# Masked attention with a residual: bulk loads and stores split over the slots, turns moved ahead, an If with its sides exchanged

## The chip, the cores and the metric

The kernel runs on one core of one Trainium2 chip, in one launch. The metric is device time in microseconds. A core has five engines that run their own instruction streams: TensorE (PE, with its weight loads as PEld), VectorE (DVE), ScalarE (ACT), GpSimd (POOL) and SyncE (SP). DMAs are issued by SP, ACT and POOL, in the order of their own streams, and moved by 16 DMA engines.

## The reference, cut to what matters

```python
def ref(x, mask, Wq, Wo):            # x (8, 512, 1024), mask (8, 1024) of 0 and 1
    NH = 8; B, D, T = x.shape; dk = D // NH
    xt = transpose(x, (0, 2, 1))
    q = xt @ Wq.T
    qh = q.reshape(B, T, NH, dk).transpose(0, 2, 1, 3)
    scores = einsum('bhqd,bhkd->bhqk', qh, qh) / sqrt(dk)
    logits = (scores * cmask + (1 - cmask) * -1e30) * rmask
    attn = softmax(logits)
    ctx = einsum('bhqk,bhkd->bhqd', attn, qh)
    out = ctx.transpose(0, 2, 1, 3).reshape(B, T, D) @ Wo.T
    return x + transpose(out, (0, 2, 1))
```

Queries, keys and values are the same projection. About half of the 1024 tokens of each batch are kept by the mask. A row that is masked out has equal logits everywhere, so its attention is the mean over all tokens.

## The kernel before, in words

Only the kept tokens are worked on. `early()` ranks the tokens by prefix sums of the mask and finds for each place of a packed list which token goes there. A value read from the chip (`fit`, the largest number of places that a batch needs) chooses a side of an If: `late(SHORT)` for up to 544 places, `late(LONG)` for up to 576. This input takes the short side. (Behind both stands another If with a slow version for all tokens, which is not entered.)

`late(n)` is one long schedule written out by hand. The work is cut into 32 pairs `(b, pr)`: batch b = 0 to 7 and four pairs of heads pr = 0 to 3. Each pair has five steps k = 0 to 4, one block of keys each; below, a slot (pr, k) of batch b is that step. In each slot TensorE does the scores of one block and then whatever the dictionaries and `slots_of` put there: the projection of a later pair, the attention of the pair before, blocks of the output projection. The order of the calls in the source is the order of the instructions on each engine, so a DMA's place in the source fixes its place on the issuing engine's queue, not its time.

What a batch needs beside the matmuls, and where it stood before:

- `load_batch(b + 2)`, L378: x as eight pieces of 256 KB in two tiles (tag `x`, two buffers), all on SP at slot (3, 0) of batch b.
- `turn(b + 1, i)`, L426 and L434: VectorE transposes a quarter of x to rows of tokens (`xt`, two buffers); four stores on SP put it to the DRAM tile `xd`. Slots (0, 0), (0, 1), (0, 3), (1, 0) of batch b.
- `add_features`, `mean_of`: ScalarE and VectorE sum x for the mean.
- `search(b + 2, i)`, `load_ranks`: which tokens are kept. `gather(b + 1, i)`, L494: GpSimd fetches the kept rows from `xd` into `xin`, slots (1, 3) and (1, 4). `collect`, L507: TensorE transposes them to `xc` at (2, 1) and (2, 2).
- `invert`, L728 to L753, at k = 0 of every pair: VectorE inverts the sums of the softmax (`rt`), four tiny stores `row<-rt` on SP, then two loads `rb<-row` on SP that wait for those stores. `contexts`, L763 to L772, multiplies with `rb` on VectorE at k = 4.
- `lengths_of` (`len`, `top`, VectorE, L586 and L593) and `bias_of` (L599 to L604, TensorE and VectorE): the largest length of the keys, needed before the next pair's scores can be exponentiated.
- `output`, L787: the output projection; `oc` goes by GpSimd to the DRAM tile `od`.
- `load_rest(b - 1)`, L857: x once more for the residual (`xr`, 2 MB in four DMAs of 512 KB, one buffer), on SP at (3, 4); at (2, 4) in the last batch.
- `fetch`, L899, and `finish_blocks`, L862 and L865: rows of `od` come back in token order, are transposed on VectorE and added to `xr`. After block 7 (and after block 3 for batch 6) the finished `xr` is stored to `out`, L872.

`issue_stores()` at the end of each slot issues the stores of `turn` at once and those of `finish_blocks` one slot later. The last batch's end is `fetch_last` and `finish_tokens`.

Of the kernel before, what the change touches and what calls it, by code (L numbers as in the profile page):

```python
# [10 lines left out]
F32 = mybir.dt.float32  # L11
# [10 lines left out]
Q = 32  # L22
SHORT = 544
# [282 lines left out]
def attention_of_kept_tokens(ctx, tc, x, mask, wq, wo, out, ident, wqT, woT, verdict, flag):  # L306


    nc = tc.nc
    B, D, T = x.shape  # L310
    P = 128
    DK = D // NH
    SCALE = 1.0 / math.sqrt(DK)
    ND = D // P
# [53 lines left out]
    xs, xbars, xmeans, xds, xins, xcs, parts, searches = {}, {}, {}, {}, {}, {}, {}, {}  # L368
    stores = [[], []]

    def load_batch(b, queue=None):

        features = x[b].rearrange("(p d) t -> d p t", d=ND)
        xs[b] = []
        for r in range(NN):
            xs[b].append(sb.tile([P, ND, NB], F32, tag="x", name=f"x_{b}_{r}", bufs=NN))
            for d in range(ND):
                (queue or nc.sync).dma_start(  # L378
                    xs[b][r][:, d, :], features[d][..., r * NB : (r + 1) * NB]
                )  # L380

    def queries_of(b):

# [11 lines left out]
    def turn_first(i):  # L395

        r, at = divmod(i * P, NB)
        pt = bank(f"xt_0_{i}")
        for d in range(ND):
            nc.tensor.transpose(pt[:, d * P : (d + 1) * P], xs[0][r][:, d, at : at + P], ident)  # L400
        if i == 0:
            xds[0] = dr.tile([T + 1, D], F32, tag="xd_0", name="xd_0", bufs=1)
            nc.gpsimd.dma_start(xds[0][T : T + 1, :], zero)
        tag = "oc" if i < NC else "xin"
        xt = sb.tile([P, D], F32, tag=tag, name=f"xt_0_{i}", bufs=NC)
        nc.scalar.copy(
            xt.rearrange("p (a d f) -> p a d f", a=A, d=ND),
            pt.rearrange("p (d a f) -> p a d f", d=ND, a=A),
        )
        nc.gpsimd.dma_start(xds[0][i * P : (i + 1) * P, :], xt)  # L410

    def mean_first():
        xbars[0] = keep.tile([P, ND, NN], F32, name="xbar_0")
# [359 lines left out]


    ods, gs, xrs = {}, {}, {}
    copies = []

    def output(b, i, wait=False):
        n = sizes[i]
# [71 lines left out]
    def in_blocks(t):  # L851
        return t.rearrange("(k f) (a n) -> a f k n", f=Q, a=A)

    def load_rest(b):
        xr = sb.tile([P, D // Q, T // A], F32, tag="xr", name=f"xr_{b}", bufs=1)
        for a in range(A):
            nc.sync.dma_start(xr[a * Q : (a + 1) * Q, :, :], in_blocks(x[b])[a])  # L857
        xrs[b] = xr

    def finish_blocks(b, i):  # L860
        o = sb.tile([P, D // Q, Q], F32, tag="o", name=f"o_{b}_{i}", bufs=2)
        nc.vector.transpose(o.rearrange("p k t -> p (k t)"), gs[b, i])  # L862
        xr = xrs[b]
        to = xr[:, :, i * Q : (i + 1) * Q]
        nc.vector.tensor_tensor(to, o, to, ALU.add)  # L865
        n = NT if b + 2 < B else G
        if (i + 1) % n == 0:
            cols = slice((i + 1 - n) * Q, (i + 1) * Q)

            def store():  # L870
                for a in range(A):
                    nc.sync.dma_start(  # L872
                        in_blocks(out[b])[a][:, :, cols], xr[a * Q : (a + 1) * Q, :, cols]
                    )

            stores[0].append(store)

    def fetch_last(b):

# [126 lines left out]
    def early():  # L1006
# [98 lines left out]
        mean_first()  # L1105
        for i in range(NC):
            search(0, i)
    def place_all():

        BC = B * NT  # L1110
        mrow, rank = seen["mrow"], seen["rank"]
        home, wrap = homes
        nc.vector.tensor_scalar(home, rank, float(-NK), None, ALU.add)
        nc.vector.tensor_tensor(home, home, mrow, ALU.mult)
        nc.vector.tensor_scalar(home, home, float(NK - 1 + END), None, ALU.add)
        nc.vector.tensor_scalar(wrap, home, float(NK), float(-NK), ALU.is_ge, ALU.mult)
        nc.vector.tensor_tensor(home, home, wrap, ALU.add)
# [8 lines left out]
    def late(n):  # L1126
        fit_to(n)
        nc.vector.tensor_scalar(lacks, kept, float(-NK), None, ALU.add)
        weights["wq"] = order_columns(load_weights(wq, "wq"), "wq")
        mean_of(0)  # L1130
        for i in range(NC):
            gather(0, i)
        queries_of(0)
# [16 lines left out]
        bias_of(pairs[0])  # L1150


        TURN = [(0, 0), (0, 1), (0, 3), (1, 0)]
        TURN_LATER = [(0, 2), (0, 4), (1, 0), (1, 1)]
        FEATURES = {(r, k): (r * G + k - 1, *((r * G + 3,) if k == 3 else ())) for r in range(NN) for k in (1, 2, 3)}
        SEARCH = {(2, 1): (0,), (2, 2): (1,), (2, 3): (2,), (2, 4): (3,), (3, 0): (4,)}
# [23 lines left out]
        FETCH_SOON = {**FETCH, (1, 3): (6,), (1, 4): (7,), (2, 0): (), (2, 1): ()}  # L1180
        FINISH_SOON = {**FINISH, (1, 4): (6, 7), (2, 2): (), (2, 3): ()}
        FETCH_LAST = {(2, k): (k,) for k in range(NC)} | {(3, k): (NC + k,) for k in range(NT - NC)}
        FINISH_LAST = {(3, 2): (0, 1), (3, 3): (2, 3), (3, 4): (4,)}
        for p, pair in enumerate(pairs):
            b, pr = pair
            before = pairs[p - 1] if p else None
            todo = slots_of(p)
            for k, c in enumerate(order):
                scores(pair, c)
                if k == (4 if p == ND - 1 else 3) and p + 1 < len(pairs):  # L1190
                    bias_of(pairs[p + 1])
                if k == 0 and p + 1 < len(pairs) and pairs[p + 1] in turned:
                    copy_values(pairs[p + 1])
                if k == 0:
                    for copy in copies:
                        copy()
                    copies.clear()
                if k == 1:
                    add_ends(pair)
                if k == 0 and before:  # L1200
                    if p + 1 < len(pairs):
                        invert(before)
                    else:
                        inv = inverses(before)
                if p + 1 == len(pairs):
                    if k == 1:
                        spread(before, inv)
                        contexts(before)
                elif k == 4 and before:
                    contexts(before)  # L1210
                if b + 1 < B:
                    at = TURN if b else TURN_LATER
                    if (pr, k) in at:
# [12 lines left out]
                if b + 2 < B:  # L1226
                    if pr == 3 and k == 0:
                        load_batch(b + 2)
                    if pr == 1 and k == 4:
                        load_ranks(b + 2)  # L1230
                    for i in SEARCH.get((pr, k), ()):
                        search(b + 2, i)
                if (pr, k) == ((3, 4) if b + 1 < B else (2, 4)) and b > 0:
                    load_rest(b - 1)
                if b > 1:
                    for i in (FETCH if b + 1 < B else FETCH_SOON).get((pr, k), ()):
                        keep_step(pair, c)
                        fetch(b - 2, i)
                if b + 1 == B:
                    for i in FETCH_LAST.get((pr, k), ()):  # L1240
                        keep_step(pair, c)
                        fetch(b - 1, i)
                if p == 0 and k == 1:
                    place_all()
                if p == 1 and k == 4:
                    turn_places()
                if p == ND - 1 and k < 2:
                    place_blocks(k)
                if b > 1:
                    for i in (FINISH if b + 1 < B else FINISH_SOON).get((pr, k), ()):  # L1250
                        finish_blocks(b - 2, i)
                if b + 1 == B:
                    for i in FINISH_LAST.get((pr, k), ()):
                        finish_blocks(b - 1, i)
                for task in todo[k]:
                    task()
                issue_stores()
            if p + 2 == len(pairs):
                attend_short(pair)
                for hf in range(2):  # L1260
                    attend_half(pair, hf)
# [50 lines left out]
def kernel(  # L1312
# [22 lines left out]
    with ExitStack() as pools:  # L1335
# [3 lines left out]
        with tc.manual_schedule():  # L1339
            early()  # L1340
        fit = nc.values_load(verdict[0:1, 0:1], min_val=0, max_val=2 * T)
        with tc.If(fit < SHORT) as short:
            with tc.manual_schedule():
                late(SHORT)
        with short.Else():
            with tc.If(fit < LONG):
                with tc.manual_schedule():
                    late(LONG)
    again = nc.values_load(flag[0:1, 0:1], min_val=0, max_val=1)
    with tc.If(again > 0):  # L1350
        turn_all_weights(tc, [(wq, wqT), (wo, woT)], ident)
# [29 lines left out]
```

## Time and profile before

| | |
|---|---|
| median of 3 runs | 726.82 us (723.42 to 730.56) |
| the profiled execution | 729.98 us, span 728.3 us, mean clock 0.949 |
| TensorE busy | 654.2 us, 90% of the span |
| VectorE, ScalarE, GpSimd busy | 359.2 us, 398.5 us, 184.4 us |
| moved by DMA | 116.43 MB, mean 160 GB/s |

The page of the profile cuts the span into 40 slices; a digit is the busy share of an engine in tenths. The view of waits lists which engine and line stood idle until which other instruction had ended: us in total, times, longest. The chain that ended last gives pieces in order of time: start, us, what. The timeline gives start, us, engine, line, operation and, in brackets, the idle time before it and what ended that. The view of windows gives for each stretch its length, the busy time (and count) of PE, PEld, DVE, ACT and POOL, the granted clock, the busy share of the DMA engines and GB/s. SPq is the queue of SyncE's DMA issues.

### The profile page before, as it was taken

How to read it: one execution, taken by the hardware profiler on the slowest of the kernel's cores; microseconds unless marked ns; L12 is line 12 of the kernel's file. 1: busy time of each engine (PE TensorE's matmuls, PEld its weight loads, DVE VectorE, ACT ScalarE, POOL GpSimd, SP SyncE). 2: the span in 40 equal slices, each digit the busy share in tenths (PEclk: the TensorE clock that was granted, in tenths of full speed). 3: DMA queues.
4: the chain of work that ended last, by engine and by line, in shares of the span. 5: the costliest groups of instructions: out<-in, count | busy, mean ns of one | idle time of the engine just before them, and what ended most of it. 6: DMA issues, size and time to landing. Idle time of an engine off the chain costs nothing.

```text
span 728.3 us, 12025 instructions
## 1 busy us (share of the span) xinstructions
PE 654.2 (90%) x4139; PEld 397.0 (55%) x4139; DVE 359.2 (49%) x1049; ACT 398.5 (55%) x1059; POOL 184.4 (25%) x311
## 2 busy tenths in 40 slices
PE   6689999999999995899959999699987999999962
PEld 5656666565556553565535656356554655554431
DVE  6147646253575434564364632935437333723461
ACT  5457678465765566265653558356682555544400
POOL 4620310310343013330224104240132301333040
PEclk9789999999999999799989999899998999999975
DMA  8463344517753786437864488645973384329656
GB/s 289 141 185 77 109 136 106 152 38 217 196 178 99 194 202 192 134 100 211 193 201 137 126 225 201 174 128 131 243 212 93 109 195 121 92 96 248 155 174 186
DMA packets 96750, 116.43 MB, mean 160 GB/s; under 512 B 10343, under 2 KB 74343, under 8 KB 96670
## 3 DMA queue, kind: packets, MB, share of 16 engines
q1 hardware_dynamic: 79566, 74.08, 39.3%
q0 software_dynamic: 12880, 39.30, 17.2%
q10 hardware_dynamic: 4224, 2.10, 1.0%
q8 instruction: 36, 0.59, 0.4%
q14 instruction: 44, 0.36, 0.2%
HBM read 72.78 MB, written 42.67 MB: 159 GB/s over the span
## 4 chain that ended last, share of the span: by engine, by line
PE 72%; DMA 10%; DVE 8%; SPq 4%; ACT 3%; issue 2%; POOL 0%; DVEq 0%; ACTq 0%; POOLq 0%
PE s L620 16%; PE pq L538 15%; PE av L666 15%; PE po L787 13%; DMA row<-rt 5%; PE xc L507 3%; DMA xd<-xt 2%; PE s L642 2%; SPq L434 2%; PE v L563 2%; PE pa L815 2%; ACT e L628 1%; DVE xt L426 1%; DVE xr L865 1%; DMA g<-od,origin 1%
## 5 line engine op out<-in xcount | busy, mean ns | idle before, releaser
L628 ACT ACTIVATE e<-s,bias 128x544 f32<-128x544 f32 x256 | 180.6, 710 | 69.2 <-PE s L620 62.9
L620 PE MATMUL s<-qT 64*128 64x272 f32 x1024 | 171.1, 418 | 2.9 <-ACT e L628 1.7
L620 PEld LDWEIGHTS s<-qT 64*128 64x128 f32 x1024 | 98.1, 186 | 70.8 <-issue 28.0
L538 PE MATMUL pq<-xc,wqT 128*128 128x272 f32 x512 | 131.8, 413 | 0.0
L666 PE MATMUL av<-e,v 128*64 128x272 f32 x1024 | 131.4, 399 | 0.0
L538 PEld LDWEIGHTS pq<-xc,wqT 128*128 128x128 f32 x512 | 102.4, 206 | 21.1 <-issue 0.8
L787 PE MATMUL po<-woT,cT 128*128 128x512 f32 (+1 forms) x448 | 107.5, 434 | 0.0
L666 PEld LDWEIGHTS av<-e,v 128*64 128x64 f32 x1024 | 67.9, 136 | 56.0 <-issue 23.1
L799 POOL DMA_DIRECT2D od<-oc x56 | 30.4, 556 | 245.4 <-ACT oc L797 226.9
L546 ACT COPY qT<-pq 128x272 f32<-128x272 f32 x64 | 24.5, 383 | 89.5 <-PE pq L538 89.5
L787 PEld LDWEIGHTS po<-woT,cT 128*128 128x128 f32 (+1 forms) x448 | 46.8, 150 | 47.0 <-issue 46.2
L899 POOL DMA_INDIRECT g<-od,block_origin x56 | 56.2, 1003 | 39.7 <-issue 19.3
L426 DVE STREAM_TRANSPOSE xt<-x 128x1024 f32<-128x1024 f32 x28 | 34.8, 1243 | 44.6 <-DMA xd<-xt 43.9
L494 POOL DMA_INDIRECT xin<-xd,source x40 | 39.3, 982 | 64.2 <-DMA rank<-ranks 40.2
L645 ACT ACTIVATE el<-s,bias 128x544 f32<-128x544 f32 x32 | 22.9, 715 | 59.6 <-PE s L642 44.8
L657 DVE CUSTOM_DVE_ANT_0 junk<-el,part 128x272 f32<-128x272 f32 x64 | 28.2, 441 | 54.9 <-ACT el L645 43.2
L586 DVE TENSOR_REDUCE len<-sq 128x10 f32<-128x640 f32 x32 | 26.1, 816 | 54.4 <-ACT sq L584 54.4
L862 DVE STREAM_TRANSPOSE o<-g 128x512 f32<-128x512 f32 x56 | 39.2, 701 | 22.6 <-DMA g<-od,block_origin 22.5
L628 ACT ACTIVATION_READ_ACCUMULATOR e<-s,bias 128x1 f32 x256 | 50.2, 196 | 0.0
L895 POOL COPY step<-e 1x1 f32<-1x1 f32 x77 | 16.0, 208 | 125.3 <-ACT e L628 124.7
L601 DVE TENSOR_REDUCE m<-top 128x1 f32<-128x128 f32 x32 | 9.3, 290 | 71.5 <-PE top L599 71.5
L865 DVE TENSOR_TENSOR xr<-o,xr 128x512 f32<-128x512 f32 x56 | 38.8, 692 | 9.6 <-DMA xr<-in_x_dram 7.8
(148 smaller groups left out, 680.5 us busy)
## 6 DMA issues: line engine op xcount, KB each, us to landing
x<-in_x_dram SPq DMA_DIRECT2D x56, 256.0 KB
xd<-xt SPq DMA_DIRECT2D x112, 128.0 KB
xr<-in_x_dram SPq DMA_DIRECT2D x28, 512.0 KB
out_dram<-xr SPq DMA_DIRECT2D x24, 512.0 KB
rb<-row SPq DMA_DIRECT2D x60, 160.0 KB
od<-oc POOLq DMA_DIRECT2D x28, 256.0 KB
rank<-ranks SPq DMA_DIRECT2D x6, 512.0 KB
xd<-xt POOLq DMA_DIRECT2D x8, 256.0 KB
```

Source lines behind the costliest of these rows:

```text
L426: nc.vector.transpose(xt.rearrange("p k (d f) -> p k d f", d=ND), xs[b][r][:, :, at : at + n].rearrange("p d (k t) -> p k d t", t=Q),)
L494: nc.gpsimd.indirect_dma_start(out=xin[:n, :], out_offset=None, in_=xds[b], in_offset=bass.IndirectOffsetOnAxis(ap=searches[b][2][:n, i : ...
L538: nc.tensor.matmul(pq[:, :KH], wqT[:, d, pr * P : (pr + 1) * P], xcs[b][:, d, cols], start=(d == 0), stop=(d == ND - 1),)
L620: nc.tensor.matmul(ss[h][:, hf, :KH], qT[heads[h], keys], qT[heads[h], queries[hf]], start=True, stop=True,)
L628: nc.scalar.activation(e[:, :, h, :], ss[h][:, :, :KH], AF.Exp, bias=bias, scale=SCALE, accum_out=sums[pair[1] % 2][:, h, c : c + 1],)
L657: nc.vector.tensor_tensor_reduce(junk[:, :KH], e[:, 0, h, :], parts[b], 1.0, 0.0, ALU.mult, ALU.add, ends[pr % 2][:, h : h + 1])
L666: nc.tensor.matmul(av[head, :KH], v[keys, c, head], e[keys, hf if c < LAST else 0, h, :], start=(c == first), stop=(c == last),)
L787: nc.tensor.matmul(po[k * n : (k + 1) * n, :w], cTs[b, pr][:, i * P : i * P + n], woT[:, pr, k * w : (k + 1) * w], start=(pr == 0), stop=( ...
L799: nc.gpsimd.dma_start(ods[b][places[i], k * w : (k + 1) * w], oc[k * n : (k + 1) * n, :w])
L862: nc.vector.transpose(o.rearrange("p k t -> p (k t)"), gs[b, i])
L865: nc.vector.tensor_tensor(to, o, to, ALU.add)
L899: nc.gpsimd.indirect_dma_start(out=g, out_offset=None, in_=ods[b], in_offset=bass.IndirectOffsetOnAxis(ap=block_origin[:, b, i : i + 1], a ...
```

## The change

- x of batch b + 2 is loaded a piece at a time: pieces 0 to 3 at (1, 3) and (1, 4), 4 to 7 at (2, 0) to (2, 3).
- Its first two turns are at (3, 1) and (3, 3) of batch b; the other two at (0, 0) and (0, 2) of batch b + 1. Batch 1 is still turned in batch 0.
- `xr` is loaded a piece at a time at (3, 2), (3, 3), (3, 4) and (0, 0) of the next batch; in the last batch at (2, 3), (2, 4), (3, 0), (3, 1).
- The four stores of a whole batch's output go to a list `rests`, of which each slot issues one.
- In the last batch `finish_blocks` of blocks 0 and 1 is at (3, 3), of 2 to 4 at (3, 4).
- At the start the stores of `xd` for batch 0 move from GpSimd to SyncE, the loads of wq from SyncE to GpSimd, and `mean_of(0)` stands before the If.
- The outer If asks `fit > SHORT - 1`: the long side stands first in the code, the short one behind it.

```diff
+    def load_piece(b, i, queue=None):
+        r, d = divmod(i, ND)
+        if i == 0:
+            xs[b] = []
+        if d == 0:
+            xs[b].append(sb.tile([P, ND, NB], F32, tag="x", name=f"x_{b}_{r}", bufs=NN))
+        (queue or nc.sync).dma_start(
+            xs[b][r][:, d, :],
+            x[b].rearrange("(p d) t -> d p t", d=ND)[d][..., r * NB : (r + 1) * NB],
+        )
...
-            nc.gpsimd.dma_start(xds[0][T : T + 1, :], zero)
+            nc.sync.dma_start(xds[0][T : T + 1, :], zero)
...
-        nc.gpsimd.dma_start(xds[0][i * P : (i + 1) * P, :], xt)
+        nc.sync.dma_start(xds[0][i * P : (i + 1) * P, :], xt)
...
-    def load_rest(b):
-        xr = sb.tile([P, D // Q, T // A], F32, tag="xr", name=f"xr_{b}", bufs=1)
-        for a in range(A):
-            nc.sync.dma_start(xr[a * Q : (a + 1) * Q, :, :], in_blocks(x[b])[a])
-        xrs[b] = xr
+    def load_rest(b, a):
+        if a == 0:
+            xrs[b] = sb.tile([P, D // Q, T // A], F32, tag="xr", name=f"xr_{b}", bufs=1)
+        nc.sync.dma_start(xrs[b][a * Q : (a + 1) * Q, :, :], in_blocks(x[b])[a])
...
-            def store():
-                for a in range(A):
-                    nc.sync.dma_start(
-                        in_blocks(out[b])[a][:, :, cols], xr[a * Q : (a + 1) * Q, :, cols]
-                    )
-            stores[0].append(store)
+            def store(a):
+                nc.sync.dma_start(
+                    in_blocks(out[b])[a][:, :, cols], xr[a * Q : (a + 1) * Q, :, cols]
+                )
+            for a in range(A):
+                if n == NT:
+                    rests.append(lambda a=a: store(a))
+                else:
+                    stores[0].append(lambda a=a: store(a))
...
-        weights["wq"] = order_columns(load_weights(wq, "wq"), "wq")
-        mean_of(0)
+        weights["wq"] = order_columns(load_weights(wq, "wq", nc.gpsimd), "wq")
...
-        TURN = [(0, 0), (0, 1), (0, 3), (1, 0)]
+        TURN = [(3, 1), (3, 3), (0, 0), (0, 2)]
+        LOAD = {(1, 3): (0, 1), (1, 4): (2, 3), (2, 0): (4,), (2, 1): (5,), (2, 2): (6,), (2, 3): (7,)}
...
-        FINISH_LAST = {(3, 2): (0, 1), (3, 3): (2, 3), (3, 4): (4,)}
+        FINISH_LAST = {(3, 3): (0, 1), (3, 4): (2, 3, 4)}
+        REST = {(3, 2): (0,), (3, 3): (1,), (3, 4): (2,)}
+        REST_LAST = {(2, 3): (0,), (2, 4): (1,), (3, 0): (2,), (3, 1): (3,)}
...
                 if b + 2 < B:
-                    if pr == 3 and k == 0:
-                        load_batch(b + 2)
+                    if pr == 3 and (pr, k) in TURN:
+                        turn(b + 2, TURN.index((pr, k)))
+                    for i in LOAD.get((pr, k), ()):
+                        load_piece(b + 2, i)
...
-                if (pr, k) == ((3, 4) if b + 1 < B else (2, 4)) and b > 0:
-                    load_rest(b - 1)
+                if b > 1 and (pr, k) == (0, 0):
+                    load_rest(b - 2, A - 1)
+                if b > 0:
+                    for i in (REST if b + 1 < B else REST_LAST).get((pr, k), ()):
+                        load_rest(b - 1, i)
...
                 issue_stores()
+                if rests:
+                    rests.popleft()()
...
-        with tc.If(fit < SHORT) as short:
-            with tc.manual_schedule():
-                late(SHORT)
-        with short.Else():
+        with tc.If(fit > SHORT - 1) as over:
             with tc.If(fit < LONG):
                 with tc.manual_schedule():
                     late(LONG)
+        with over.Else():
+            with tc.manual_schedule():
+                late(SHORT)
```

More of the change, by code (lines that the diff above doesn't have):

```diff
@@ L369, in attention_of_kept_tokens @@
     stores = [[], []]
-    def load_batch(b, queue=None):
[L373 to L379, printed above, removed]
-                )
+    def load_piece(b, i, queue=None):
[8 more added lines that the diff above has]
+        )
+    def load_batch(b, queue=None):
+        for i in range(NN * ND):
+            load_piece(b, i, queue)
     def queries_of(b):
@@ L775, in attention_of_kept_tokens @@
     ods, gs, xrs = {}, {}, {}
-    copies = []
+    copies, rests = [], deque()
     def output(b, i, wait=False):
@@ L868, in finish_blocks @@
             cols = slice((i + 1 - n) * Q, (i + 1) * Q)
-            def store():
-                for a in range(A):
-                    nc.sync.dma_start(
-                        in_blocks(out[b])[a][:, :, cols], xr[a * Q : (a + 1) * Q, :, cols]
-                    )
-            stores[0].append(store)
+            def store(a):
[7 more added lines that the diff above has]
+                    stores[0].append(lambda a=a: store(a))
     def fetch_last(b):
@@ L1107, in early @@
             search(0, i)
+        mean_of(0)
     def place_all():
@@ L1212, in late @@
                     at = TURN if b else TURN_LATER
-                    if (pr, k) in at:
+                    if pr < 2 and (pr, k) in at:
                         turn(b + 1, at.index((pr, k)))
```

## The prediction

> **What bounds the kernel now.** I read the page first: its span, the busy slices of TensorE and the granted clock.
>
> ```profile
> span 728.3 us, 12025 instructions
> PE   6689999999999995899959999699987999999962
> PEclk9789999999999999799989999899998999999975
> ```
>
> TensorE is full in most slices, so an engine beside it only matters where the PE row dips. Apart from the start and the end it dips four times, some 90 us apart, and the clock falls there too. The view of waits names what TensorE waited for, and the longest wait of VectorE:
>
> ```profile
> PE top L599 <- DVE top L593: 33.5, 5, 10.6
> ...
> DVE xt L426 <- DMA xd<-xt: 43.9, 6, 12.5
> ```
>
> 33.5 us of waiting on VectorE's `top`, 10.6 at the longest. The chain that ended last gives the period of a batch: one output block of 40 matmuls falls at slot (1, 4) of each batch from b=1 to b=6 (a slot (pr, k) is pair pr, step k).
>
> ```profile
> 139.92 4.45 PE po L787 x40
> ...
> 216.23 4.45 PE po L787 x40
> ...
> 305.53 4.45 PE po L787 x40
> ...
> 391.65 4.45 PE po L787 x40
> ...
> 476.97 4.45 PE po L787 x40
> ...
> 562.09 4.45 PE po L787 x40
> ```
>
> The distances are 76.3, 89.3, 86.1, 85.3 and 85.1 us. The first is a batch without a dip; the other four lose 13.0 + 9.8 + 9.0 + 8.8 = 40.6 us. The timeline of SyncE's queue and of VectorE through one dip shows why:
>
> ```profile
> 236.04 5.28 SPq L872 DMA_DIRECT2D out_dram<-xr  x4
> ...
> 250.47 3.86 SPq L378 DMA_DIRECT2D x<-in_x_dram  x8
> 254.37 4.74 SPq L857 DMA_DIRECT2D xr<-in_x_dram  x4
> 259.56 6.45 SPq L748 DMA_DIRECT2D row<-rt  x4
> 273.59 1.09 SPq L753 DMA_DIRECT2D rb<-row  x2
> ...
> 275.25 10.42 SPq L434 DMA_DIRECT2D xd<-xt  x12
> ```
>
> ```profile
> 258.10 0.21 DVE L745 STREAM_TRANSPOSE rt<-ris 128x32 f32<-128x32 f32 x1
> ...
> 282.12 1.25 DVE L426 STREAM_TRANSPOSE xt<-x 128x1024 f32<-128x1024 f32 x1 [12.49 <-DMA xd<-xt]
> ...
> 293.79 0.16 DVE L593 TENSOR_REDUCE top<-len 128x1 f32<-128x10 f32 x1
> ```
>
> SyncE runs ahead of the slots: the 2 MB of x written at (3, 0) and the 2 MB of xr written at (3, 4) go out together from 250.47 to 259.1. The tiny `row` of slot (0, 0), ready at 258.31, is issued behind them and its readers `rb` follow only at 273.59, 15.3 us after it was ready. The stores of `xt` stand behind `rb` on the same queue; VectorE's third turn needs one of two `xt` buffers back and waits 12.49 us; everything of VectorE behind it, down to `top` at 293.79, is late, and TensorE stands. It also comes back slowly. The same 16 projection matmuls, undisturbed and after each of the four dips:
>
> ```profile
> 156.40 3.67 PE pq L538 x16
> ...
> 294.48 5.80 PE pq L538 x16
> ...
> 381.37 5.03 PE pq L538 x16
> ...
> 466.69 5.04 PE pq L538 x16
> ...
> 551.60 5.25 PE pq L538 x16
> ```
>
> 2.1 + 1.4 + 1.4 + 1.6 = 6.4 us of slow matmuls, and 33.5 + 6.4 = 39.9, so the 40.6 is accounted for twice.
>
> **The change part by part.** (1) *The loads and the turns.* The eight x pieces leave (3, 0) for (1, 3) to (2, 3), three of the four xr pieces stand at (3, 2), (3, 3), (3, 4), the fourth at (0, 0), and two of four turns move to (3, 1) and (3, 3) of the batch before. No transfer is added; bytes and piece sizes stay. What counts is the order on SyncE's queue. Before the `row` of (0, 0) there then stand, from the last VectorE work it waits for (the turn at (3, 3)), four `xd` stores of 128 KB and one xr piece of 512 KB: 1 MB instead of 4 MB.
>
> ```profile
> 263.00:267.00 4.00, 4.00 (x34) 2.32 (x32) 1.38 (x3) 3.47 (x11) 1.72 (x3) 1.00 1.11 214
> ```
>
> Within the burst the windows show the DMA engines full (share 1.11) at 214 GB/s, so 1 MB is an estimated 4.9 us and 4 MB 19.6. The 1 MB is issued about two slots (2 x 76.3/20 = 7.6 us) ahead, so `row` should meet a nearly empty queue. And a bound from the other side, the boundary into b=2, where the stores of 236.04 do not exist yet and the same 4 MB are issued earlier:
>
> ```profile
> 181.94 1.41 SPq L748 DMA_DIRECT2D row<-rt  x4
> 188.46 1.09 SPq L753 DMA_DIRECT2D rb<-row  x2
> ```
>
> There `rb` comes 6.5 us after `row`, and its batch is the one of 76.3 us: 6.5 us of delay is still free. The third turn, at (0, 0), now reuses the buffer of the turn at (3, 1), whose stores were put on the queue four slots (15 us) earlier and not behind this `rb`, so its 12.49 us go as well. Bounds: half of the 40.6 stays if `row` is late by half (rival A), and nothing more than 40.6 is to be had, since outside the dips the PE row shows TensorE full. I take the whole 40.6, because the 1 MB in front of `row` is far nearer to the boundary into b=2 than to the four late ones.
>
> (2) *A new wait.* The output stores go out one a slot from (2, 3) to (3, 1), and the first xr piece at (3, 2) refills their buffer, so SyncE waits there for the last of them to land. Behind it stand the second xr piece, the stores of the turn at (3, 3), the third piece and `row`. From the `rb` of (3, 0) on there are two of the stores and the stores of one turn, 1.5 MB or 7.4 us at 214 GB/s, and (3, 0) to (0, 0) is five slots, 19 us; some 10 us of cover are left for what stands behind. If that cover were gone, `row` would be late again, which is the first rival. In the last batch one store of 512 KB (2.4 us) now goes ahead of a `row`; the 6.5 us above cover that.
>
> (3) *The end.* In the last batch `finish_blocks` of blocks 2, 3 moves from (3, 3) to (3, 4). Its 1 MB store was issued at the end of (3, 4); now nothing issues it before the very last call, behind the `od` stores:
>
> ```profile
> 685.80 2.82 SPq L872 DMA_DIRECT2D out_dram<-xr  x4
> 695.91 4.07 SPq L840 DMA_DIRECT2D od<-oc  x5
> 703.70 12.94 SPq L872 DMA_DIRECT2D out_dram<-xr  x4
> ```
>
> ```profile
> 684.00:688.00 4.00, 4.00 (x17) 1.41 (x18) 3.73 (x10) 2.23 (x6) 0.00 (x0) 1.00 0.28 69
> 688.00:692.00 4.00, 4.00 (x46) 2.54 (x44) 1.57 (x7) 1.19 (x3) 0.00 (x0) 1.00 0.75 197
> ...
> 700.00:704.00 4.00, 0.00 (x0) 0.00 (x0) 3.86 (x9) 0.00 (x0) 2.89 (x4) 0.68 0.74 227
> ```
>
> Where it lay it used (0.28 + 0.75) x 4 = 4.1 us of all DMA engines, under a busy TensorE. At 700 it meets the final gathers and stores, with (1 - 0.74) x 4 = 1.0 us free in that window. Bounds 0 and +4.1, taken +3.
>
> (4) *The start.* The `xd` stores of batch 0 move to SyncE and wq to GpSimd; the same 5 MB are moved.
>
> ```profile
> 18.00:20.00 2.00, 0.00 (x0) 0.00 (x0) 1.97 (x6) 2.00 (x3) 0.00 (x0) 0.69 0.09 35
> ...
> 20.29 1.06 POOL L494 DMA_INDIRECT xin<-xd,source  x1 [4.87 <-DVE source L485]
> ```
>
> The DMA engines fall quiet at about 18.2 and the first gather starts at 20.29, about 2.1 us behind the last byte. Shorter by all of it: -2.1; as much longer if wq, now behind GpSimd's branch, is last: +2.1. I take -0.5. `mean_of(0)` moved ahead of the branch is hidden behind this gather.
>
> By the Trainium skill (Runtime: NRT & Kernel Launch, Instruction fetch mechanics) a taken branch to a far target breaks the sequential prefetch and the engine stalls for a fetch. The exchanged sides would put such a jump on every engine at the start and take one away at the end, and no row of before prices one. By the rows the start is hidden behind the 4.87 us for which GpSimd stands before its first gather, and the sum below stays 692.4; by the rule a fetch longer than that would push the gather, and the end would be shorter by one fetch.
>
> (5) *Batch 0* gets 1 MB of x on the queue near its gathers, which have the least room of all:
>
> ```profile
> 72.68 1.08 POOL L494 DMA_INDIRECT xin<-xd,source  x1 [0.96 <-PE av L666]
> ```
> ```profile
> 79.43 1.09 PE L507 MATMUL xc<-ident,xin 128*128 128x128 f32 x8
> ```
>
> 6.8 us from gather to use. Bounds 0 and the whole 4.9 us of that 1 MB; taken +0.5, since x goes out a few us before.
>
> Sum against the profiled execution of 729.98 us (span 728.3 and 1.7 around it): -40.6 + 3 - 0.5 + 0.5 = -37.6, so 692.4. That run lies 3.2 us above the median of 726.82. If its excess was in the dips, 692.4 stands; if elsewhere, it is 689.2. I take 691.
>
> **The rivals.** *A, half a dip stays.* The wait of (2) outlasts its cover, `row` is late by half of what it was. For it: SyncE stops at one wait with everything behind it. Against: about 10 us of cover. 729.98 - 20.3 + 3 = 712.7, or 709.5 from the median: 711.
>
> *B, it does not do what it says.* SyncE ran ahead of the slots in the rows above, so "a piece a slot" is not kept: four x pieces and the ranks leave together after the `rb` of (1, 0), four more after that of (2, 0). If these bursts hold up the rows there as the old one did, the dips move and keep their size: 729.98 + 3, some 730 to 733. Against: 1 to 1.5 MB, an estimated 5 to 7 us, with a whole pair (19 us) until the next row.
>
> *C, slower.* The gathers of the next batch now share the middle of each batch with x, and TensorE waits at `xc` of (2, 1).
>
> ```profile
> 217.28 1.01 POOL L494 DMA_INDIRECT xin<-xd,source  x1 [0.54 <-PE po L787]
> ```
> ```profile
> 229.58 1.82 PE xc L507 x16
> ```
>
> The price of a missed use is a dip of the old size, 40.6/4 = 10.2 us, in six batches (0 to 5, those that load x): 729.98 - 40.6 + 3 + 61 = 753. It decides once the gathers take over 12.3 us; the x burst beside them is 4.9 us. Little speaks for it.
>
> **How the numbers follow.** A measurement of this kernel tells about 1% from no change. The forecast has 0.80: its ends are -40.6 - 2.1 from the median's side (684) and -40.6 + 4.1 + 2.1 + 4.9 from the profiled run (700). A has 0.12, B 0.04, C 0.04. To leave no more than 2 in 10 outside I go two us towards A: 684 to 702. Faster: forecast and A, 0.92; within 1%: B, 0.04; slower: C, 0.04.
>
> **What would show it right or wrong.** Right: `PE top <- DVE top` falls from 33.5 to under 3 us; the blocks of 40 matmuls stand 76 to 77 us apart throughout; `rb` follows the `row` of (0, 0) within 7 us; VectorE's wait for `xd<-xt` is nearly gone; eight output stores stand behind `od` at the end, which is 1 to 4 us longer from the last `po` on. Wrong: distances of 80 us or more (A, B), or a TensorE wait at `xc` (C).

## The result and the profile after

| | before | changed |
|---|---|---|
| median (runs) | 728.29 us (4; 723.42 to 730.56) | 687.42 us (4; 685.61 to 689.28) |
| the profiled execution, its span | 729.98 us, 728.3 us | 688.52 us, 686.8 us |
| mean clock | 0.949 | 0.971 |
| TensorE busy, share of the span | 654.2 us, 90% | 644.3 us, 94% |

The ratio of the times is 0.9447 with a 95% interval of 0.9388 to 0.9507: 5.5% faster. The forecast was 691.0 us, 684 to 702. Lines have moved by 5 behind the new `load_piece`, and a little more further down: L599 is now L604, L787 is L792, L748 and L753 are L753 and L758.

From the page of the changed kernel, the span, the row of TensorE and the granted clock:

```profile
span 686.8 us, 12034 instructions
...
PE   6489999999999999999999999999999999999952
...
PEclk9698999999999999999999999999999999999976
```

The four dips are gone from both rows; the start has a weaker slice (4) than before. From the view of waits (us in total, times, longest):

```profile
PE xc L512 <- DMA xin<-xd,source: 5.6, 1, 5.6
...
PE top L604 <- DVE top L598: 0.8, 1, 0.8
```

The wait at `top` fell from 33.5 to 0.8 us (the 0.8 stands at the start in both kernels), and no wait of VectorE for `xd<-xt` is left in the view (43.9 before). The blocks of 40 matmuls and one undisturbed projection from the chain that ended last:

```profile
34.24 3.88 PE pq L543 x16
...
142.38 4.45 PE po L792 x40
...
218.37 4.45 PE po L792 x40
...
294.35 4.45 PE po L792 x40
...
310.50 3.67 PE pq L543 x16
...
370.35 4.45 PE po L792 x40
...
446.45 4.45 PE po L792 x40
...
522.45 4.45 PE po L792 x40
...
654.03 4.82 PE po L836 x10
```

The distances are 76.0, 76.0, 76.0, 76.1 and 76.0 us, and the projection after a batch's boundary takes 3.67 us again. Cut at these pieces, the two spans compare so:

| stretch | before | after | difference |
|---|---|---|---|
| start of the span to the first `pq` | 30.40 | 34.24 | +3.8 |
| first `pq` to the block of b=1 | 109.52 | 108.14 | -1.4 |
| block of b=1 to that of b=6 | 422.17 | 380.07 | -42.1 |
| block of b=6 to the last `po` | 132.01 | 131.58 | -0.4 |
| last `po` to the end of the span | 34.2 | 32.8 | -1.4 |
| span | 728.3 | 686.8 | -41.5 |

So the five batches between gave 42.1 us and the start took back 3.8. The timeline of SyncE's queue at the boundary that was shown of before:

```profile
251.21 0.47 SPq L875 DMA_DIRECT2D out_dram<-xr  x1
255.84 0.85 SPq L862 DMA_DIRECT2D xr<-in_x_dram  x2
256.79 2.26 SPq L439 DMA_DIRECT2D xd<-xt  x4
259.09 1.05 SPq L862 DMA_DIRECT2D xr<-in_x_dram  x1
260.18 5.01 SPq L753 DMA_DIRECT2D row<-rt  x4
267.98 1.09 SPq L758 DMA_DIRECT2D rb<-row  x2
...
283.56 1.95 SPq L378 DMA_DIRECT2D x<-in_x_dram  x4
```

```profile
267.54 1.25 DVE L431 STREAM_TRANSPOSE xt<-x 128x1024 f32<-128x1024 f32 x1
272.23 0.23 DVE L768 TENSOR_TENSOR rb<-rb 128x64 f32<-128x64 f32 x1 [0.85 <-DMA rb<-row]
```

`rb` follows `row` after 7.8 us instead of 14.0, the third turn (267.54) waits for nothing, and the new wait on the last output store is there: SyncE stands from 251.68 to 255.84, 4.2 us. Then three xr pieces and the stores of one turn, 2 MB, go out in 4.3 us, and SyncE reaches `row` 0.1 us after its `rt` is ready (260.06). The x loads still leave four at a time (283.56): SyncE runs ahead of the slots as before, only elsewhere.

### The profile page after: what moved, and what is told of

Read it like the earlier page. It is cut to its first block, busy times and chain, and to the rows that moved or that the text cites. A ratio compares the mean times of both kernels' runs of the same rounds, so it can differ in the third digit from the quotient of the medians.

```text
span 686.8 us, 12034 instructions
## 1 busy us (share of the span) xinstructions
PE 644.3 (94%) x4139; PEld 391.8 (57%) x4139; DVE 359.6 (52%) x1049; ACT 398.1 (58%) x1059; POOL 181.8 (26%) x306
## 4 chain that ended last, share of the span: by engine, by line
PE 90%; DMA 3%; ACT 2%; DVE 1%; issue 1%; POOL 1%; POOLq 0%; ACTq 0%
PE s L625 23%; PE av L671 21%; PE pq L543 17%; PE po L792 15%; PE s L647 3%; PE xc L512 3%; PE v L568 2%; PE pa L820 2%; DMA xd<-xt 1%; PE top L604 1%; ACT e L633 1%; DMA g<-od,origin 1%; PE po L836 1%; PE xt L405 1%; DMA xin<-xd,source 0%
## 5 line engine op out<-in xcount | busy, mean ns | idle before, releaser
L543 PE MATMUL pq<-xc,wqT 128*128 128x272 f32 x512 | 125.2, 398 | 0.0
L543 PEld LDWEIGHTS pq<-xc,wqT 128*128 128x128 f32 x512 | 97.6, 196 | 19.0 <-issue 0.8
L792 PE MATMUL po<-woT,cT 128*128 128x512 f32 (+1 forms) x448 | 107.5, 434 | 0.0
L804 POOL DMA_DIRECT2D od<-oc x56 | 30.2, 551 | 248.9 <-ACT oc L802 248.7
L792 PEld LDWEIGHTS po<-woT,cT 128*128 128x128 f32 (+1 forms) x448 | 46.8, 150 | 47.0 <-issue 46.2
L499 POOL DMA_INDIRECT xin<-xd,source x40 | 39.1, 978 | 22.9 <-DMA xd<-xt 8.6
L487 DVE TENSOR_SCALAR_CACHE_REDUCE junk<-rank,key 128x1024 f32<-128x1024 f32 (+4 forms) x40 | 40.0, 1000 | 3.4 <-ACT rank L1092 2.5
```

Of the source, the lines that this page charges most:

```text
L487: nc.vector.tensor_scalar(junk[:, :n], rank[:, i * P :], key[:, col], 0.0, ALU.is_le, ALU.add, accum_out=found[:, col])
L499: nc.gpsimd.indirect_dma_start(out=xin[:n, :], out_offset=None, in_=xds[b], in_offset=bass.IndirectOffsetOnAxis(ap=searches[b][2][:n, i : ...
L543: nc.tensor.matmul(pq[:, :KH], wqT[:, d, pr * P : (pr + 1) * P], xcs[b][:, d, cols], start=(d == 0), stop=(d == ND - 1),)
L792: nc.tensor.matmul(po[k * n : (k + 1) * n, :w], cTs[b, pr][:, i * P : i * P + n], woT[:, pr, k * w : (k + 1) * w], start=(pr == 0), stop=( ...
L804: nc.gpsimd.dma_start(ods[b][places[i], k * w : (k + 1) * w], oc[k * n : (k + 1) * n, :w])
```

## The experiments

Each stands beside runs of the kernel before on its own chip, so ratios to that are compared.

### Which part removes the dips

*loads_only* is the kernel before with the first two items of the change alone: x a piece a slot, turns moved. The diff is against the kernel before; the dictionaries are those of the change.

```diff
...
-                    if pr == 3 and k == 0:
-                        load_batch(b + 2)
+                    if pr == 3 and (pr, k) in TURN:
+                        turn(b + 2, TURN.index((pr, k)))
+                    for i in LOAD.get((pr, k), ()):
+                        load_piece(b + 2, i)
```

> The kernel before with one part of the change: x a piece a slot and the turns moved; xr in one burst at (3, 4), output stores in one burst, start and If as before. Theory Q (the order on SyncE's queue: the row of (0, 0) stands behind what was issued before it, and its delay reaches TensorE through the xt buffers): 2.5 MB instead of 4 MB stand in front of the row, and the third turn no longer waits for stores behind rb; rb comes about 272 to 274 on the clock of the profile before, just in time, so the dips shrink to 0 to 3 us each: 690 to 702 us, and VectorE's wait for xd<-xt falls from 43.9 to under 5 us. Rival X (the xr burst is what counts): dips stay, above 715. Rival V (volume: any 2 MB burst costs half a dip): about 708.

Measured: 687.36 us, ratio 0.9461 (0.9363 to 0.9559). It does as much as the whole change, and better than expected. Its `row` still waits behind 2 MB of xr:

```profile
252.15 2.26 SPq L862 DMA_DIRECT2D xr<-in_x_dram  x4
255.18 1.56 SPq L753 DMA_DIRECT2D row<-rt  x4
266.01 1.09 SPq L758 DMA_DIRECT2D rb<-row  x2
```

That is 10.8 us to `rb`, and the periods are 76.0, 76.0, 76.0, 77.3 and 76.0 us: 10.8 us are just in time. In the batch of 77.3 us `rb` followed `row` after 12.4 us (407.20 to 419.63).

*rest_only* is the other part: xr and the stores a piece a slot and the late last store, with x and the turns as before. The diff is against the changed kernel; the start and the If, also as before, are left out.

```diff
-        TURN = [(3, 1), (3, 3), (0, 0), (0, 2)]
-        LOAD = {(1, 3): (0, 1), (1, 4): (2, 3), (2, 0): (4,), (2, 1): (5,), (2, 2): (6,), (2, 3): (7,)}
+        TURN = [(0, 0), (0, 1), (0, 3), (1, 0)]
+        LOAD = {(3, 0): tuple(range(8))}
...
```

> The kernel before with the other part of the change: xr and the output stores a piece a slot (with the later blocks at the end); x in one burst at (3, 0) and the turns at (0, 0), (0, 1), (0, 3), (1, 0) as before. Theory Q: the stores and xr pieces now stand among the x burst in front of the row of (0, 0), 4 MB or more, and the third turn still waits for stores behind rb: dips stay, 715 to 735 us, VectorE's wait for xd<-xt above 30 us. Rival X (xr is what counts): 690 to 695. Rival V: about 708.

Measured: 726.36 us, ratio 0.9935 (0.9903 to 0.9966). The waits are those of before:

```profile
DVE xt L431 <- DMA xd<-xt: 39.8, 6, 10.0
PE top L604 <- DVE top L598: 31.6, 6, 8.0
```

The distances are 76.0, 86.7, 86.2, 85.0 and 85.7 us: spreading xr and the stores removes no dip while the x burst stands in front of the turns.

*x_only* parts the two items of loads_only: x a piece a slot, turns where they were.

```diff
...
-                    if pr == 3 and k == 0:
-                        load_batch(b + 2)
+                    for i in LOAD.get((pr, k), ()):
+                        load_piece(b + 2, i)
```

> The kernel before with only the x loads a piece a slot; the turns stay at (0, 0), (0, 1), (0, 3), (1, 0), xr in one burst. Theory Q (what stands in front of the row decides): 2 MB of xr go out right behind the rb of (3, 0), the row of (0, 0) lands some 10 us earlier than before and with it the turn's stores, so the third turn waits 0 to 4 us and the dips shrink to 0 to 3 us each: 688 to 700 us. Rival M (moving the turns away from behind rb is what counts): dips of 7 us and more stay, above 712 us.

Measured: 687.69 us, ratio 0.9462 (0.9412 to 0.9511), the same as loads_only, with distances of 76.0, 76.0, 76.0, 77.4 and 76.0 us. The x loads alone carry the gain, and the rival that gives it to the turns' new places falls. SyncE's queue and the third turn, still in its old slot and its old buffer:

```profile
248.60 2.73 SPq L861 DMA_DIRECT2D xr<-in_x_dram  x4
256.51 1.41 SPq L752 DMA_DIRECT2D row<-rt  x4
262.09 1.09 SPq L757 DMA_DIRECT2D rb<-row  x2
...
263.76 8.12 SPq L438 DMA_DIRECT2D xd<-xt  x12
```

```profile
268.69 1.25 DVE L430 STREAM_TRANSPOSE xt<-x 128x1024 f32<-128x1024 f32 x1 [0.89 <-DMA xd<-xt]
```

With 2 MB less in front, `rb` comes 5.6 us after `row`, the `xd` stores go out at once, and the turn waits 0.89 instead of 12.49 us.

### The two links of the chain, each by itself

*xt_three* keeps all bursts of before and gives the third turn a third buffer (one `o` buffer less, to make room).

```diff
-        xt = sb.tile([P, n // Q, P], F32, tag="xt", name=f"xt_{b}_{i}", bufs=2)
+        xt = sb.tile([P, n // Q, P], F32, tag="xt", name=f"xt_{b}_{i}", bufs=3)
...
-        o = sb.tile([P, D // Q, Q], F32, tag="o", name=f"o_{b}_{i}", bufs=2)
+        o = sb.tile([P, D // Q, Q], F32, tag="o", name=f"o_{b}_{i}", bufs=1)
```

> The kernel before with three xt buffers instead of two (and one o buffer instead of two, to make room); nothing else. Theory Q: the third turn no longer waits, VectorE next waits for rb, which lands about 276 instead of VectorE being free at 283: some 6 us less of each dip, 700 to 710 us, with 4 to 7 us of wait for rb<-row per dip. Rival R (the late row alone makes the dip, the buffer adds nothing): within 1% of before. Rival T (the buffer alone makes it): 685 to 692.

Measured: 702.03 us, ratio 0.9663 (0.9561 to 0.9764), as expected. VectorE no longer stops at the turn, but one step later at `rb`, whose `row` is as late as before:

```profile
254.38 3.77 SPq L748 DMA_DIRECT2D row<-rt  x4
267.61 1.09 SPq L753 DMA_DIRECT2D rb<-row  x2
```

```profile
265.61 1.25 DVE L426 STREAM_TRANSPOSE xt<-x 128x1024 f32<-128x1024 f32 x1
271.31 0.22 DVE L763 TENSOR_TENSOR rb<-rb 128x64 f32<-128x64 f32 x1 [4.45 <-DMA rb<-row]
```

The distances are 76.0, 80.3, 82.4, 81.9 and 77.4 us. Against loads_only on the same chip, 0.9663 to 0.9461: some 15 us of the gain hang on the lateness of `row` itself; the larger part, some 25 us, goes with the turn's wait for its buffer.

*row_on_pool* takes `row` and `rb` off the crowded queue and leaves everything else.

```diff
-            nc.sync.dma_start(
+            nc.gpsimd.dma_start(
                 row[:, :, a, :].rearrange("h c j -> (h c) j"),
...
-            nc.sync.dma_start(
+            nc.gpsimd.dma_start(
                 rb[h * DK : (h + 1) * DK, :],
```

> The kernel before with row and rb issued by GpSimd instead of SyncE; all bursts stay. Theory Q: the row no longer stands behind 4 MB on its own queue and lands within about 4 us of its rt, so contexts are in time; the stores of the turns still stand behind the burst on SyncE and the third turn still waits a little, so most of a dip goes, 3 to 5 us of each are left: 695 to 712 us. Rival B (bandwidth: the 16 DMA engines are full, whichever queue a transfer is on): the row is as late as before, 725 us or more. GpSimd stands for each row, which may hold od, g and xin up: any time above 730 is that.

Measured: 734.71 us, ratio 1.0113 (0.9925 to 1.0301): no gain, a miss. At (0, 0) the transfers do what was expected: `rt` is ready at 274.71, `row` is issued at 275.01 and `rb` at 280.03, VectorE has it at 284.91, and the third turn waits 0.96 us. But the slot (3, 0) ahead of it, whose `rt` is ready at 251.11, now meets the burst. GpSimd, SyncE's queue and VectorE:

```profile
252.25 1.08 POOL L748 DMA_DIRECT2D row<-rt  x2
255.84 1.03 POOL L748 DMA_DIRECT2D row<-rt  x2 [2.52 <-issue]
261.83 1.08 POOL L753 DMA_DIRECT2D rb<-row  x2 [4.96 <-DMA row<-rt]
```

```profile
246.53 5.24 SPq L872 DMA_DIRECT2D out_dram<-xr  x4
251.87 8.67 SPq L378 DMA_DIRECT2D x<-in_x_dram  x8
260.94 3.44 SPq L857 DMA_DIRECT2D xr<-in_x_dram  x4
```

```profile
271.01 0.23 DVE L763 TENSOR_TENSOR rb<-rb 128x64 f32<-128x64 f32 x1 [11.75 <-DMA rb<-row]
...
284.91 0.23 DVE L763 TENSOR_TENSOR rb<-rb 128x64 f32<-128x64 f32 x1 [2.47 <-DMA rb<-row]
```

SyncE no longer stops at the `rb` of (3, 0), so x and xr follow the output stores at once, and `row` and `rb` of (3, 0) are moved beside them, on another queue. VectorE gets that `rb` 19.9 us after `rt` (12.8 in before) and stands 11.75 us; at (3, 0) of b=2 to 6 it stands 11.0 to 12.2 us. In xt_three, where `row` stands behind the burst on SyncE's own queue, `rb` came 17.0 us after `rt`. So a queue of its own did not spare the tiny transfer the burst, as rival B had it; the windows show the DMA engines at a share of 0.90 to 1.12 from 249 to 275. By the Trainium skill (DMA: Bandwidth & Descriptors, Queues, rings and completion order) each DMA engine takes turns between the queue rows that have work for it, and within one row consumes in order; the 19.9 beside the 17.0 us show no gain from that here.

The dips do shrink: from the block of b=1 to that of b=6 it is 405.3 us instead of 422.2. But batch 0 takes 7.2 us more and the stretch behind the block of b=6 takes 9.5 us more. GpSimd's own waits are part of that:

```profile
POOL rb L753 <- DMA row<-rt: 98.4, 30, 7.3
DVE rb L763 <- DMA rb<-row: 97.0, 17, 13.5
POOL row L748 <- DVE rt L745: 91.1, 16, 17.8
```

In batch 0 the fourth gather stands behind a `row` and an `rb` on GpSimd: it is issued at 85.67 (76.81 in before), and TensorE waits 4.22 us for its rows at `xc` (89.30). Behind b=6 VectorE stands 13.46 us for an `rb`, and TensorE then 8.0 us.

### The start

The first gather of the changed kernel is at 24.11 instead of 20.29. Theory F: the taken jump costs each engine a fetch, at a time when the DMA engines are full, and wq now stands behind it. Theory G: the exchange of the queues of wq and `xd` does it. The changed kernel was run again beside the following three, as *again*:

> The changed kernel again, for comparison on the same chip: 685 to 690 us; first gather at about 24 us, the end after the last po about 33 us long.

Measured: 692.43 us, ratio 0.9432 (0.9384 to 0.948), with the first gather at 23.86 and 33.0 us from the last `po` to the end. The time is above the 685 to 690 expected, and so is that of before on this chip (732.92). *if_back* has the test of the If and the order of its sides as before:

```diff
-        with tc.If(fit > SHORT - 1) as over:
+        with tc.If(fit < SHORT) as short:
...
```

> The changed kernel with the If as before (short side first). Theory F (each engine loses 3 to 6 us after the taken jump at the start, and wq, which GpSimd issues behind it, is late by as much): wq is issued at about 8 instead of 13.4, the first gather comes at 20 to 21 instead of 24.1, the end grows by about 2: some 1 to 2 us faster than the changed kernel. Rival G (moving wq to GpSimd and xd to SyncE is what delays the start): gather stays at 24 and the whole is about 2 us slower.

Measured: 694.99 us, ratio 0.9488 (0.9453 to 0.9523). The rows of the start, first again, then if_back (in brackets the idle time before):

```profile
13.70 2.20 POOL L989 DMA_DIRECT2D wq<-in_L_cond_Wq_dram  x4 [7.12 <-DVE xbar L420]
...
24.26 0.17 DVE L1137 TENSOR_SCALAR lacks<-kept 128x8 f32<-128x8 f32 x1 [3.33 <-issue]
...
33.53 3.88 PE pq L543 x16
```

```profile
8.27 2.21 POOL L989 DMA_DIRECT2D wq<-in_L_cond_Wq_dram  x4 [1.66 <-DVE pads L1109]
...
21.70 0.17 DVE L1137 TENSOR_SCALAR lacks<-kept 128x8 f32<-128x8 f32 x1 [0.56 <-DVE mean L457]
...
30.81 3.88 PE pq L543 x16
```

With the sides as before, the first instruction behind the If comes 5.4 us earlier on GpSimd, with 1.66 us of idle time instead of 7.12; on VectorE with 0.56 instead of 3.33, for which nothing but its own issue accounts. The first gather is 2.4 us earlier (21.41 instead of 23.86), the first projection 2.7. In these rows the mechanism is F's; the total is not (expected 1 to 2 us faster, measured 2.6 slower), since the same edit makes the end 4.8 us longer (37.8 from the last `po` instead of 33.0), of which I had expected 2.

*queues_back* keeps the exchanged sides and gives the two queues back.

```diff
-        nc.sync.dma_start(xds[0][i * P : (i + 1) * P, :], xt)
+        nc.gpsimd.dma_start(xds[0][i * P : (i + 1) * P, :], xt)
...
-        weights["wq"] = order_columns(load_weights(wq, "wq", nc.gpsimd), "wq")
+        weights["wq"] = order_columns(load_weights(wq, "wq"), "wq")
```

> The changed kernel with the queues of the start as before (xd of batch 0 on GpSimd, wq on SyncE), If exchanged. Theory F: SyncE loses 3 to 6 us at the jump, wq is issued at 12 to 14, the gather comes at 23 to 24: within 1.5 us of the changed kernel. Rival G: gather back at 20 to 21, 3 to 4 us faster.

Measured: 691.15 us, ratio 0.9437 (0.9399 to 0.9475). wq leaves SyncE at 10.96 instead of 8.04, the first gather is at 23.09, the first projection at 32.17: still 1.8 us later than before. Going by these rows, G falls as the main cause: the queues account for 1.4 us of the start (33.53 to 32.17), the sides for 2.7.

*wq_early* loads wq on SyncE in `early()`, ahead of the If and behind the x loads, so that the jump delays no large transfer.

```diff
+        seen["wq"] = load_weights(wq, "wq")
...
-        weights["wq"] = order_columns(load_weights(wq, "wq", nc.gpsimd), "wq")
+        weights["wq"] = order_columns(raw, "wq")
```

> The changed kernel with the four wq loads on SyncE ahead of the If, behind the x loads. Theory F: the same bytes are moved as soon as before the change, xd lands near 20, the first gather comes at 20 to 21 while the jump's loss on GpSimd is hidden; 2 to 4 us faster than the changed kernel, unless ScalarE's own loss at the jump holds the ordering of wq up past 24, then 1 to 2. Rival G': gather still at 23 or later, no gain.

Measured: 689.88 us, ratio 0.9415 (0.9381 to 0.945). wq is issued at 5.40, the first gather at 20.73, the first projection at 30.24, 3.3 us earlier than again, while VectorE still stands 3.38 us behind the jump. This fits that the jump costs through what is queued behind it. Of the totals of these four only if_back and wq_early are parted by their intervals, and barely; the rest is read from the rows.

### The end

*store_early* calls `issue_stores()` once more, ahead of the last attention, so that the 1 MB of blocks 2 to 3 leaves before the `od` stores. *wq_and_store* has this and wq_early together.

```diff
         last = pairs[-1]
+        issue_stores()
         attend_last(last)
```

> The changed kernel with one more issue_stores() ahead of attend_last, so that the 1 MB of finished blocks of batch 6 goes out ahead of the od stores again. Theory (that 1 MB is 2 to 3 us of the end, and the exchanged If hides it in the total): from the last po to the end 30 to 31.5 us instead of 32.8 to 33, 1 to 3 us less in all: 684 to 689. Rival (it fits into gaps of the DMA engines): no change within 1 us.

> The changed kernel with wq loaded ahead of the If on SyncE and the finished 1 MB stored ahead of od: both mends together. First gather at 20.7 as with wq early alone, the end 30 to 32 us: 2 to 3 us below wq early alone and 4 to 5 below the changed kernel, if the two add; with nothing from the store, as wq early alone (about 2 below the changed kernel).

Measured: 682.92 us, ratio 0.9401 (0.9361 to 0.9442), and 682.77 us, 0.9398 (0.936 to 0.9437). These are the lowest medians of all, but the intervals overlap that of the changed kernel; the gain is clearer in the trace. wq_and_store, its last `po` and the last stores on SyncE's queue, against eight in one burst in the changed kernel:

```profile
649.58 4.82 PE po L836 x10
```

```profile
640.21 2.71 SPq L875 DMA_DIRECT2D out_dram<-xr  x4
...
659.18 12.66 SPq L875 DMA_DIRECT2D out_dram<-xr  x4
```

```profile
659.95 19.74 SPq L875 DMA_DIRECT2D out_dram<-xr  x8
```

From the last `po` to the end of the span the kernels fall into four groups:

| | 1 MB early | 1 MB late |
|---|---|---|
| sides as before | 34.2 before, 34.3 loads_only, 33.9 x_only, 33.4 row_on_pool, 32.8 xt_three | 37.8 if_back, 37.9 rest_only |
| sides exchanged | 30.0 store_early, 29.7 wq_and_store, 29.5 wq_burst_xr | 32.8 changed, 33.0 again, 33.5 queues_back, 34.5 wq_early |

Each figure is from one profile. The late store costs 3 to 5 us in either row, and the exchanged sides save 3 to 5 us in either column.

In store_early alone the first gather is at 19.56 and the first projection at 30.15, although the jump is where it was: there wq left at 15.06, later than in again and behind the `xd` stores, which then landed early. With the same code up to there, the changed kernel, again and store_early have their first projection at 34.24, 33.53 and 30.15, so the start varies from one execution to the next by as much as the loss of 3.8 us itself. That fits that adding wq_early brought nothing more that these runs can tell, against the 2 to 3 us expected. The differences of 1.4 to 3.3 us read from single starts above are therefore no firm prices; the three kernels with wq ahead of the If start at 30.2 to 30.9.

### The spread of xr

*wq_burst_xr* is wq_early with the third to fifth items of the change undone: xr and the stores in bursts, the 1 MB early.

```diff
...
-                if b > 1 and (pr, k) == (0, 0):
-                    load_rest(b - 2, A - 1)
-                if b > 0:
-                    for i in (REST if b + 1 < B else REST_LAST).get((pr, k), ()):
+                if (pr, k) == ((3, 4) if b + 1 < B else (2, 4)) and b > 0:
+                    for i in range(A):
                         load_rest(b - 1, i)
...
```

> As wq early alone, but xr loaded and the output stored in bursts as in the kernel before (which also brings the early store at the end back). Theory (the spread xr brings nothing in the middle): periods of 76 us with at most one of 77 to 78, the end 30 to 32 us, within 2 us of the kernel with both mends. Rival (spread xr matters once x is spread): periods of 77 to 79, 5 us or more slower.

Measured: 686.75 us (682.51 to 688.28), ratio 0.9435 (0.9383 to 0.9487). Four periods are 76.0 or 76.1 us and one is 81.1, which neither forecast had. VectorE's wait for `rb`, first here, then in wq_and_store:

```profile
DVE rb L768 <- DMA rb<-row: 21.6, 8, 7.6
```

```profile
DVE rb L768 <- DMA rb<-row: 4.1, 3, 1.5
```

Behind the xr burst `row` is just in time in four batches and late in one, where `rb` follows it after 13.0 us (484.80 to 497.81); the spread buys the margin. In the medians that is 4 us, within the intervals.

## Why the prediction was right, and where it was not

- **What bounds the kernel** and step (1): right. The dips were priced at 40.6 us and gave 42.1; the extra 1.5 us are the distances of 76.0 where I took the one undisturbed batch, 76.3, as the floor (5 x 0.3). That floor is not one of the program: in again, on another chip, the five distances are 76.3 to 76.8. The second count of the 40.6 is a little high, since 0.8 of the 33.5 us stands at the start and not in a dip: 32.7 + 6.4 = 39.1. Of the chain of `row`, `rb`, `xd` stores, turn and `top` the links were shown: xt_three cuts it at the turn and meets `rb`, x_only takes 2 MB out of the front and all of it goes. What makes `row` late was not parted: the step calls it the order on SyncE's queue, but row_on_pool, with `row` on another queue, finds it as late wherever it meets the burst (19.9 us from `rt` to `rb` in hand, 17.0 in xt_three). That the x burst must not stand just ahead of `row` is shown; whether the queue or the full DMA engines hold `row` up stays open. One part of the step was not needed: the third turn's new place and buffer, which I put beside the queue's order as a reason. x_only has neither, and the same time.
- `rb` **within 7 us**: 7.5 to 8.1 at the four boundaries. The some 10 us of cover of step (2) were used up: the output stores landed later than counted (SyncE waits 3.9 to 4.2 us for them), and it reaches `row` 0.1 to 1.4 us after its `rt` is ready. So in front of `row` stand 2 MB put out just before, not 1 MB put out two slots ahead. It cost nothing: loads_only bears 10.8 us too, and loses 1.3 us in the batch of 12.4.
- **Step (3), the late store**: +3 taken, 3 to 5 shown by the four groups. The end as a whole was 1.4 us shorter, not 1 to 4 us longer as I wrote, because the exchanged sides saved about as much or more, which the sum held at nothing.
- **Step (4), the start, is the step that failed**: -0.5 taken with bounds of 2.1 either way; +3.8 measured in the profiled execution, with single starts that vary by up to 4 us. I said that the fetch behind the taken jump hides behind the 4.87 us for which GpSimd stands before its first gather. But wq was moved to that very engine and behind that very jump: it left at 13.36 instead of 8.04, fell into the time of the `xd` stores, and the quiet of the DMA engines, from which I counted the bounds, came some 2.6 us later (about 20.8 instead of 18.2 in the windows). In store_early, where wq left behind the `xd` stores, the same start lost nothing (30.15). The bound was drawn from the bytes, as if only their order could change and not the time at which the last of them may be issued. The rule named there (the Trainium skill, Runtime: NRT & Kernel Launch, Instruction fetch mechanics) agrees in sign with the rows of the start: VectorE stood 3.3 to 4.2 us behind the jump, and GpSimd's first DMA came 5.4 us later than without it. The end is shorter too, as I drew from the rule, but no run shows that the jump is why.
- **Step (5), batch 0**: +0.5 taken, -1.4 measured. The x on the queue made no gather late, and a wait of 1.19 us at `xc` of batch 1, for ScalarE, is gone; the rest is not accounted for.
- **The rivals**: A did not come, although the cover of (2) was used up, since the 2 MB then in front of `row` were few enough. B's premise was right (x leaves four at a time) and its result was not, since no `row` is due behind those bursts. C: the only wait at `xc` is 5.6 us at the start (1.3 in before), part of (4).
- The sum of 692.4 and the 691 taken stand against 688.5 for the profiled run and 687.4 for the median: the misses of the start (+4.3) and of the end (-4.4) cancel, and the dips (-1.5), batch 0 (-1.9) and the rest (-0.4) remain. That they cancel is luck: the total is better than its parts.

## What to carry to other kernels

Look at what stands in front of a tiny transfer on its queue: 4 MB of loads issued just ahead of four stores of 1.2 KB cost 40 us over four batches here, and moving the 2 MB of x among them half a batch earlier took all of it back. Moving the tiny transfer to another queue did not do it: SyncE, no longer stopped, put the burst out earlier, another tiny transfer met it and was as late, and the gathers behind it on the issuing engine were late as well. And if a branch is turned round, ask which DMAs are issued behind it at the start: issue the large ones ahead of it.

## What the runs showed of the hardware

- Behind the taken jump VectorE was idle 3.3 to 4.2 us, with nothing else to wait for, in the seven profiles with the sides exchanged (0.56 to 0.58 us in the seven with the short side first). Why GpSimd took 5.4 us in if_back's comparison is not settled.
- With the exchanged sides the end was 3 to 5 us shorter. In before, 6.2 us lie between the last bulk transfer and the end of the span; in the changed kernel 4.3, in if_back 7.0, in store_early 3.4. That the jump at the end of the short side is what is saved fits these, but no record shows it.
- A tiny store and its reload (`row`, `rb`) beside a burst of 4 MB: 19.9 us from `rt` to use on GpSimd's queue at (3, 0), 10.2 us at the next slot (274.71 to 284.91), and 17.0 us behind such a burst on SyncE's queue in xt_three.
